# A sparse graph layer on one core: seven units multiply one dense tile of g fewer, and its columns move into their gathered lists

## The chip, the cores and the metric

The kernel runs on one NeuronCore of a Trainium2 chip. The metric is device microseconds of one execution; the kernel before takes 1518.41 us (median of 3 runs, 1517.39 to 1519.67). The engines are TensorE (PE, with its weight loads PEld), VectorE (DVE), ScalarE (ACT), GpSimd (POOL) and SyncE (SP).

## The reference

Eight batches of 4096 nodes with 256 features pass through one graph layer. The adjacency `adj` is sparse: node i is linked to node j with a probability that falls as the square root of both numbers, so the first nodes have by far the most links.

```python
HW     = einsum('bnf,fo->bno', x, W)                # 8 x 4096 x 256
A_norm = relu((adj + adj.T) * 0.5)                  # 4096 x 4096
D      = sum(A_norm, axis=1)
L_norm = eye(4096) - D**-0.5[:, None] * A_norm * D**-0.5[None, :]
out    = relu(einsum('nm,bmo->bno', L_norm, HW))
return layernorm(x + out, axis=-1)
```

The inputs come from a fixed seed, so the pattern of the adjacency is always the same one. Everything is float32.

## The kernel before

It works in two phases. In the **first phase** it reads `adj` in 512x512 tiles, symmetrises them on PE and DVE, writes the result to `a_dram`, and forms g = r * (x W), where r is the inverse root of a node's degree. g has 4096 rows of 2048 values (8 KB: eight batches times 256 features) and is written to `g_dram`. Beside this, PE multiplies row block 0 with all of g (`lead`, L584).

In the **second phase** the other 31 blocks of 128 output rows follow in 16 **units** of two blocks (unit 15 has one), in the order `SEQ` = 1 to 9, 0, 10 to 15. A unit needs only those rows of g whose node is linked to one of its 256 output rows. They are gathered:

- The first `HUBS[u]` tiles of g (a tile is 128 rows; tiles 0 and 1 are almost full) stay in SBUF as `g_hub0` and `g_hub1` and are multiplied densely, with a 128x128 piece of the adjacency that POOL loads for each block (`gh`, L1019, 64 KB).
- All other linked rows go into lists. Each node has a kind: which of the unit's eight groups of 32 output rows it is linked to. `KINDS` names 15 kinds: one group alone (eight kinds), two neighbouring groups, one whole block (15 and 240), or anything (0). `CAPS[u]` gives each kind so many half tiles of 64 places, `FIRST[u]` says where they begin. What does not fit into a kind's places moves on to the kind for pairs, for a block, and last to "anything". A place that stays free is read out of bounds and moves no data. If even that list is too short, a flag makes a complete dense recomputation follow (L1335).
- For each tile of 128 places POOL issues two gathers: the adjacency rows `ga` (L1031) and the g rows `g` (L1039). They go into a ring of 12 buffers; `gather_ahead` issues the next one when the oldest buffer has been used for the last time. Buffers come free in order.

`steps_of` (L877) is the planner for PE. A **step** is what fills the PE array once for all four 512-wide pieces of the output row: a hub tile or a tile of kind 15, 240 or 0 times one block (four full 128x128 matmuls), or a packed **round**, in which up to eight smaller products (64 rows, or 32 or 64 columns) run side by side in the array. `weave` mixes them; the first step of a unit is hub 0 for block 0, the first step of the second block is hub 0 again, and the other hub products are spread between the rounds. A float32 matmul shows as two instructions in the trace.

The queues are ordered by hand (`queue`, `tc.issue_after`). On POOL the gathers and the `gh` loads stand in the order in which the steps release their buffers. ACT evicts the finished blocks (L787) and then issues the loads of the two residual rows `xr` of the next unit (1 MB each); DVE adds, normalises and builds the lists for later units (L238 to L480), PE counts for it (L299, L396, L449), and SP stores each finished block (1 MB).

Lines that matter here: `HUBS`, `CAPS` and `FIRST` (L26 to L64), `steps_of` (L877), `load_hub_rows` (L1012), `gather` and `gather_ahead` (L1024 to L1063), the product (L1254).

Of the kernel before, what the change touches and what calls it, by code (L numbers as in the profile page):

```python
# [22 lines left out]

SEQ = [*range(1, 10), 0, *range(10, 16)]

HUBS = [2] * 16  # L26

CAPS = [
# [16 lines left out]
]  # L45
# [18 lines left out]
]  # L64
# [3 lines left out]
def kernel(  # L68
# [180 lines left out]
    def patterns(u):  # L249

        def t(shape, name, dtype=F32, **kw):
            return ipool.tile(shape, dtype, tag=name, name=f"{name}_{u}", **kw)
# [13 lines left out]
        nc.vector.tensor_tensor(diag, diag, own[:, :, :nb], ALU.max)  # L266
        if HUBS[u]:
            nc.vector.memset(used[:, :, : HUBS[u]], 0.0)
        several = t([P, NB], "several", bufs=1)
# [607 lines left out]
    def steps_of(u):  # L877
# [60 lines left out]
        def full(t, b):  # L938
            return [(t, None, b, 0, QU)]

        def weave(*several):
            several = [list(s) for s in several]
            total = [len(s) for s in several]
            out = []
            while any(several):
                at = max(range(len(several)), key=lambda k: (len(several[k]) / max(total[k], 1), total[k]))
                out.append(several[at].pop(0))
            return out

        held = range(HUBS[u])  # L950
        out = [full(-1, 0)] if HUBS[u] else []
        starts = [full(t, 0) for t in whole[15]]
# [4 lines left out]
        out += weave(rounds[:first_b1], [full(-1 - h, 0) for h in held[1:]], starts)  # L957
        out += [full(-1, 1)] if HUBS[u] else []
        rows = [[full(t, 0), full(t, 1)] for t in whole[0]]
# [13 lines left out]
    with (  # L973
# [5 lines left out]
            gath.enter_context(tc.tile_pool(name=f"hub_{h}", bufs=1)).tile([P, G], F32, name=f"g_hub{h}")  # L979
            for h in range(max(HUBS))  # L980
        ]
# [409 lines left out]
```

## Time and profile before

| | |
|---|---|
| median of 3 runs | 1518.41 us |
| the profiled execution | 1526.28 us, span 1524.6 us, mean granted PE clock 0.976 |
| first phase | up to 584.7 us (first step of unit 1 follows at 588) |
| second phase | 584.7 to 1509.8 us: 925.1 us |
| after it | 14.8 us: the last block is evicted, normalised and stored |
| PE busy | 1430.9 us, 94% of the span |
| DMA queues, share of 16 engines | 48.1% POOL (q0), 23.9% SP (q1), 22.5% ACT (q10) |

The bounds of the units are the evictions of their second blocks: unit 3 begins at 734.3, unit 9 ends at 1150.7, unit 0 lasts to 1248.1, unit 13 ends at 1441.4. In a table of stretches each row gives the length, then busy time and number of instructions of PE, PEld, DVE, ACT and POOL, the granted clock, the share of the 16 DMA engines in use and GB/s. The DMA share adds up the times of single packets and can come out a little over 1.

### The profile page before, as it was taken

Reading aid. Unit: us, or ns where it says so; the run is one execution under the profiler, and the core shown is the slowest. Engines: PE = TensorE matmul, PEld = TensorE weight load, DVE = VectorE, ACT = ScalarE, POOL = GpSimd, SP = SyncE. Lnnn points to the kernel's source line nnn. Section 1 sums busy time; section 2 is a strip of 40 time slices with the busy share of each in tenths; the row PEclk is TensorE's granted clock in tenths of the full one; section 3 lists DMA queues with packets and bytes.
Section 4 is the critical chain, followed back from the end, with each engine's and each line's share of the span. In section 5 each row is a group of like instructions: output and inputs, shape, how many; then the busy total and the mean of one; then the engine's idle time right before and its main releaser. Section 6 shows DMA issues by size and latency. Waiting matters only on the chain.

```text
span 1524.6 us, 20569 instructions
## 1 busy us (share of the span) xinstructions
PE 1430.9 (94%) x6768; PEld 759.5 (50%) x6768; DVE 1028.0 (67%) x3010; ACT 369.3 (24%) x462; POOL 744.7 (49%) x1547
## 2 busy tenths in 40 slices
PE   7999988989999999989999989998999999989996
PEld 6777867777777753333333333332333333333332
DVE  5677569789597726074757676886799149879544
ACT  4555544544455430000000101010100010101102
POOL 3444010012133327556667565576476635756663
PEclk9999999989999999999999989999999999999998
DMA  9999999998999999888989899999899969998996
GB/s 349 364 371 387 405 364 363 386 362 329 393 358 326 371 418 362 337 320 328 358 304 371 288 396 348 356 383 413 294 382 358 412 206 372 364 347 299 405 396 236
DMA packets 215264, 540.52 MB, mean 355 GB/s; under 512 B 17750, under 2 KB 107526, under 8 KB 180838
## 3 DMA queue, kind: packets, MB, share of 16 engines
q0 software_dynamic: 53808, 281.94, 48.1%
q1 hardware_dynamic: 93200, 126.62, 23.9%
q10 hardware_dynamic: 68144, 130.58, 22.5%
q8 instruction: 56, 0.92, 0.2%
q14 instruction: 56, 0.46, 0.1%
HBM read 425.72 MB, written 136.34 MB: 369 GB/s over the span
## 4 chain that ended last, share of the span: by engine, by line
PE 64%; DVE 14%; DMA 14%; issue 3%; ACT 2%; POOL 1%; another core or an unknown queue 1%; ACTq 0%; DVEq 0%; POOLq 0%
PE py L1254 46%; PE pg L626 8%; DMA a_dram<-sym 7%; PE lead L584 5%; DVE sym L519 4%; DMA xin<-in_x_dram 4%; DMA g<-g_dram,gi 2%; PE xtr L615 2%; PE tr L515 2%; ACT sym L523 1%; DVE sums L526 1%; DVE stats L806 1%; DVE xr L797 1%; PE lists L449 1%; DVE xr L830 1%
## 5 line engine op out<-in xcount | busy, mean ns | idle before, releaser
L1254 PE MATMUL py<-g,ga 128*32 128x512 f32 (+4 forms) x2880 | 651.4, 604 | 16.3 <-issue 11.4
L1254 PEld LDWEIGHTS py<-g,ga 128*32 128x32 f32 (+4 forms) x2880 | 230.5, 138 | 408.3 <-issue 389.8
L1039 POOL DMA_INDIRECT g<-g_dram,gi x256 | 288.9, 1128 | 164.3 <-issue 74.3
L1031 POOL DMA_INDIRECT ga<-a_dram,ai x256 | 271.7, 1061 | 159.4 <-issue 59.9
L787 ACT ACTIVATE y<-py,minus_r 128x512 f32<-128x512 f32 x120 | 81.0, 687 | 824.7 <-PE py L1254 598.8
L1254 PE MATMUL py<-g_hub,gh 128*128 128x512 f32 x496 | 234.5, 614 | 13.5 <-DVE low L464 6.6
L626 PE MATMUL pg<-w_sb,xt 128*128 128x256 f32 x1024 | 231.7, 385 | 7.9 <-ACT xt L616 7.7
L626 PEld LDWEIGHTS pg<-w_sb,xt 128*128 128x128 f32 x1024 | 195.8, 194 | 35.5 <-ACT xt L616 8.7
L519 DVE TENSOR_TENSOR sym<-tr,adj 128x512 f32<-128x512 f32 x256 | 162.2, 683 | 60.6 <-PE tr L515 51.1
L526 DVE TENSOR_REDUCE sums<-sym 128x64 f32<-128x2048 f32 x64 | 145.5, 2279 | 64.4 <-ACT sym L523 64.4
L1254 PEld LDWEIGHTS py<-g_hub,gh 128*128 128x128 f32 x496 | 92.3, 194 | 142.3 <-issue 127.2
L527 POOL TENSOR_SCALAR uses<-sums 128x64 uint8<-128x64 f32 x64 | 26.7, 417 | 268.4 <-DVE sums L526 234.9
L515 PE MATMUL tr<-ident,adj 128*128 128x128 f32 x1024 | 137.7, 282 | 19.2 <-DVE sym L519 14.0
L523 ACT ACTIVATE sym<-sym 128x2048 f32<-128x2048 f32 x64 | 122.7, 1918 | 122.4 <-DVE sym L519 118.3
L515 PEld LDWEIGHTS tr<-ident,adj 128*128 128x128 f32 x1024 | 115.6, 143 | 50.4 <-DVE sym L519 31.5
L241 DVE TENSOR_TENSOR_SCAN incl_r<-carry,lists 128x32 f32<-128x32 bf16 x13 | 2.9, 220 | 164.9 <-PE lists L396 164.9
L428 DVE TENSOR_TENSOR hot<-iota_q,at 128x1024 bf16<-128x1024 f32 x64 | 74.6, 1219 | 33.9 <-ACT y L787 32.1
L797 DVE TENSOR_TENSOR xr<-xr,y 128x2048 f32<-128x2048 f32 x31 | 70.8, 2284 | 38.9 <-ACT y L787 34.3
L615 PE MATMUL xtr<-ident,xin 128*128 128x128 f32 x512 | 71.9, 291 | 18.9 <-DVE sym L519 9.8
L830 DVE TENSOR_SCALAR xr<-xr,mv,root 128x256 f32<-128x256 f32 x248 | 84.3, 412 | 1.1
L806 DVE BATCH_NORM_STATS2 stats<-xr 128x6 f32<-128x256 f32 x248 | 84.0, 412 | 1.1
L584 PE MATMUL lead<-gt,strip 128*128 128x512 f32 x176 | 82.4, 593 | 0.0
(164 smaller groups left out, 1038.4 us busy)
## 6 DMA issues: line engine op xcount, KB each, us to landing
adj<-in_adj_dram SPq DMA_DIRECT2D x64, 1024.0 KB
a_dram<-sym ACTq DMA_DIRECT2D x64, 1024.0 KB
out_dram<-xr SPq DMA_DIRECT2D x31, 1024.0 KB
xr<-in_x_dram ACTq DMA_DIRECT2D x28, 1024.0 KB
xin<-in_x_dram SPq DMA_DIRECT2D x44, 512.0 KB
g_dram<-gt ACTq DMA_DIRECT2D x22, 1024.0 KB
xin<-in_x_dram POOLq DMA_DIRECT2D x20, 512.0 KB
g_dram<-held ACTq DMA_DIRECT2D x10, 1024.0 KB
```

What stands on the lines that cost most here:

```text
L515: ins = nc.tensor.transpose(pt[:, c * P : (c + 1) * P], tji[:, c, a * P : (a + 1) * P], ident)
L519: nc.vector.tensor_add(sym[:, a, :], pt, tij[:, a, :])
L523: nc.scalar.activation(sym, sym, AF.Relu, scale=0.5)
L526: nc.vector.tensor_reduce(sums, sym.rearrange("p a (c q) -> p a c q", q=E), AX.X, ALU.add)
L584: nc.tensor.matmul(lead[c], lhsT=strip, rhs=g[:, c * S : (c + 1) * S], start=not done, stop=len(done) == NB - 1, skip_group_check=True,)
L615: nc.tensor.transpose(pt[:, k, c, :], xin[b // H][:, b % H + k, c * P : (c + 1) * P], ident)
L626: ins = nc.tensor.matmul(pg[:, k * FO : (k + 1) * FO], lhsT=xt[:, b + k, c, :], rhs=w_sb[:, c, :], start=(c == 0), stop=(c == FC - 1),)
L806: nc.vector.bn_stats(stats[:, b, :], z[:, b, :])
L830: nc.vector.tensor_scalar(z[:, b, :], z[:, b, :], mv[:, b, 0:1], rstd[:, b : b + 1], ALU.subtract, ALU.mult,)
L1031: nc.gpsimd.indirect_dma_start(out=at if both else at[:, : E if one else P], out_offset=None, in_=a_pairs if both else a_groups if one els ...
L1039: nc.gpsimd.indirect_dma_start(out=gt, out_offset=None, in_=g_dram, in_offset=bass.IndirectOffsetOnAxis(ap=gi[:, t : t + 1], axis=0), boun ...
L1254: return nc.tensor.matmul(py[2 * u + 1 + b][c][cols, :], lhsT=at[ps, off + cols.start : off + cols.stop], rhs=gt[ps, c * S : (c + 1) * S], ...
```

## The change

Only three tables differ. `HUBS` is 1 instead of 2 for units 3, 7, 8, 10, 11, 12 and 13: their two products with `g_hub1` (one for each block) go, and so do the `gh` loads for them. The rows of g in tile 1 that these units need go into the lists, and `CAPS` and `FIRST` of the seven units are laid out anew. Nothing else of the program is edited; the planner draws up the steps, the gathers and the queues from the tables.

```diff
@@ -23,23 +23,23 @@
 
 SEQ = [*range(1, 10), 0, *range(10, 16)]
 
-HUBS = [2] * 16
+HUBS = [2, 2, 2, 1, 2, 2, 2, 1, 1, 2, 1, 1, 1, 1, 2, 2]
 
 CAPS = [
     [5, 4, 4, 4, 4, 2, 2, 2, 2, 3, 2, 2, 2, 2, 12],
     [3, 3, 3, 3, 3, 3, 3, 3, 3, 3, 2, 2, 2, 2, 6],
     [2, 3, 3, 3, 3, 3, 3, 3, 3, 2, 2, 2, 2, 2, 4],
-    [2, 3, 3, 2, 3, 3, 3, 2, 3, 2, 2, 2, 2, 2, 4],
+    [3, 3, 3, 2, 2, 3, 3, 2, 2, 3, 2, 2, 2, 2, 4],
     [2, 3, 3, 2, 3, 3, 3, 3, 2, 2, 2, 2, 2, 2, 2],
     [4, 2, 2, 2, 2, 2, 2, 2, 2, 2, 2, 2, 2, 2, 2],
     [1, 2, 2, 2, 2, 2, 2, 2, 2, 1, 2, 2, 2, 2, 4],
-    [2, 3, 2, 2, 3, 3, 2, 2, 3, 2, 2, 2, 0, 2, 2],
+    [2, 4, 4, 4, 4, 2, 2, 2, 2, 2, 0, 0, 2, 2, 4],
+    [2, 2, 2, 2, 2, 2, 2, 2, 2, 2, 2, 2, 2, 2, 2],
+    [2, 2, 2, 2, 2, 2, 2, 2, 2, 2, 2, 2, 0, 2, 2],
     [0, 2, 2, 2, 2, 2, 2, 2, 2, 2, 2, 2, 2, 0, 4],
+    [0, 2, 2, 2, 2, 2, 2, 2, 2, 2, 2, 2, 2, 2, 2],
     [2, 2, 2, 2, 2, 2, 2, 2, 2, 2, 2, 2, 0, 2, 2],
-    [1, 2, 2, 2, 2, 2, 2, 2, 2, 1, 2, 2, 2, 2, 2],
-    [1, 3, 3, 3, 3, 3, 3, 3, 3, 1, 0, 0, 0, 0, 4],
-    [1, 3, 3, 3, 3, 3, 3, 3, 3, 1, 0, 0, 0, 0, 4],
-    [1, 2, 2, 2, 2, 2, 2, 2, 2, 1, 2, 2, 0, 2, 2],
+    [3, 2, 2, 2, 2, 2, 2, 2, 2, 3, 0, 0, 0, 0, 4],
     [2, 2, 2, 2, 2, 2, 2, 2, 2, 2, 0, 0, 0, 0, 4],
     [6, 2, 2, 2, 2, 0, 0, 0, 0, 0, 0, 0, 0, 0, 0],
 ]
@@ -48,17 +48,17 @@
     [0, 8, 16, 12, 20, 32, 36, 34, 38, 5, 24, 26, 28, 30, 40],
     [24, 0, 12, 6, 18, 3, 15, 9, 21, 27, 30, 32, 34, 36, 38],
     [32, 0, 12, 6, 18, 3, 15, 9, 21, 34, 24, 26, 28, 30, 36],
-    [30, 0, 6, 18, 12, 3, 9, 28, 15, 32, 20, 22, 24, 26, 34],
+    [12, 0, 6, 18, 20, 3, 9, 30, 32, 15, 22, 24, 26, 28, 34],
     [30, 0, 6, 18, 12, 3, 15, 9, 28, 32, 20, 22, 24, 26, 34],
     [24, 0, 4, 2, 6, 16, 20, 18, 22, 28, 8, 10, 12, 14, 30],
     [0, 2, 6, 4, 8, 18, 22, 20, 24, 1, 10, 12, 14, 16, 26],
-    [26, 0, 14, 12, 6, 3, 24, 22, 9, 28, 16, 18, 0, 20, 30],
+    [28, 0, 8, 4, 12, 20, 24, 22, 26, 30, 0, 0, 16, 18, 32],
+    [24, 0, 4, 2, 6, 16, 20, 18, 22, 26, 8, 10, 12, 14, 28],
+    [22, 0, 4, 2, 6, 14, 18, 16, 20, 24, 8, 10, 0, 12, 26],
     [0, 0, 4, 2, 6, 14, 18, 16, 20, 22, 8, 10, 12, 0, 24],
+    [0, 0, 4, 2, 6, 16, 20, 18, 22, 24, 8, 10, 12, 14, 26],
     [22, 0, 4, 2, 6, 14, 18, 16, 20, 24, 8, 10, 0, 12, 26],
-    [0, 2, 6, 4, 8, 18, 22, 20, 24, 1, 10, 12, 14, 16, 26],
-    [24, 0, 12, 6, 18, 3, 15, 9, 21, 25, 0, 0, 0, 0, 26],
-    [24, 0, 12, 6, 18, 3, 15, 9, 21, 25, 0, 0, 0, 0, 26],
-    [0, 2, 6, 4, 8, 16, 20, 18, 22, 1, 10, 12, 0, 14, 24],
+    [0, 6, 10, 8, 12, 14, 18, 16, 20, 3, 0, 0, 0, 0, 22],
     [16, 0, 4, 2, 6, 8, 12, 10, 14, 18, 0, 0, 0, 0, 20],
     [8, 0, 4, 2, 6, 0, 0, 0, 0, 0, 0, 0, 0, 0, 0],
 ]
```

What the tables make of it, by running the planner on both and by counting the links of the reference's adjacency (rows: linked rows of g that are gathered, out of the places of the unit's tiles):

| unit | steps before, now | of them hub | tiles | rows gathered |
|---|---|---|---|---|
| 3 | 17, 16 | 4, 2 | 19, 19 | 2128, 2248 |
| 7 | 14, 13 | 4, 2 | 16, 18 | 1874, 1976 |
| 8 | 14, 12 | 4, 2 | 14, 15 | 1778, 1880 |
| 10 | 13, 12 | 4, 2 | 14, 14 | 1680, 1775 |
| 11 | 12, 11 | 4, 2 | 15, 14 | 1594, 1688 |
| 12 | 12, 11 | 4, 2 | 15, 14 | 1569, 1664 |
| 13 | 12, 11 | 4, 2 | 13, 13 | 1537, 1632 |
| all 16 | 234, 226 | 62, 48 | 256, 257 | 29952, 30655 |

No list of either kernel is too long for its places (the tightest, "anything" of unit 11, holds 127 of 128), so the dense recomputation runs in neither.

On PE, unit 13 shows it. Before, after the first round on gathered tiles, the step with hub tile 1 stands ahead of the first step of the second block (`py_0` is the unit's first block, `py_1` its second; the index behind it is one of the four 512-wide pieces):

```order
L1254 MATMUL py_0_3_11760<-g_5771,ga_5783 32x512
L1254 MATMUL py_0_0_11757<-g_hub_5723,gh_0_5786 128x512
L1254 MATMUL py_0_1_11758<-g_hub_5723,gh_0_5786 128x512
L1254 MATMUL py_0_2_11759<-g_hub_5723,gh_0_5786 128x512
L1254 MATMUL py_0_3_11760<-g_hub_5723,gh_0_5786 128x512
L1254 MATMUL py_1_0_11850<-g_hub_5719,gh_1_5785 128x512
L1254 MATMUL py_1_1_11851<-g_hub_5719,gh_1_5785 128x512
L1254 MATMUL py_1_2_11852<-g_hub_5719,gh_1_5785 128x512
L1254 MATMUL py_1_3_11853<-g_hub_5719,gh_1_5785 128x512
```

Now a step with a gathered tile of a whole block stands there:

```order
L1254 MATMUL py_0_3_11672<-g_5713,ga_5758 32x512
L1254 MATMUL py_0_0_11669<-g_5717,ga_5759 128x512
L1254 MATMUL py_0_1_11670<-g_5717,ga_5759 128x512
L1254 MATMUL py_0_2_11671<-g_5717,ga_5759 128x512
L1254 MATMUL py_0_3_11672<-g_5717,ga_5759 128x512
L1254 MATMUL py_1_0_11765<-g_hub_5705,gh_1_5771 128x512
L1254 MATMUL py_1_1_11766<-g_hub_5705,gh_1_5771 128x512
L1254 MATMUL py_1_2_11767<-g_hub_5705,gh_1_5771 128x512
L1254 MATMUL py_1_3_11768<-g_hub_5705,gh_1_5771 128x512
```

The step that needed no gather is gone; the one in its place needs the fifth gather of the unit.

On POOL, at the first gathers of unit 13 (the rows of `g` and `ga` with `gi` 11309 before, 11224 now, behind the last of unit 12), stands before:

```order
L1031 DMA ga_5779<-a_dram,ai_10872 128x32
L1039 DMA g_5755<-g_dram,gi_10870 128x2048
L1031 DMA ga_5780<-a_dram,ai_11311 128x32
L1039 DMA g_5759<-g_dram,gi_11309 128x2048
L1019 DMA gh_0_5786<-a_dram 128x128
L1019 DMA gh_1_5785<-a_dram 128x128
L1031 DMA ga_5781<-a_dram,ai_11311 128x32
L1039 DMA g_5763<-g_dram,gi_11309 128x2048
```

and now:

```order
L1031 DMA ga_5766<-a_dram,ai_10836 128x32
L1039 DMA g_5745<-g_dram,gi_10834 128x2048
L1031 DMA ga_5767<-a_dram,ai_11226 128x32
L1039 DMA g_5749<-g_dram,gi_11224 128x2048
L1031 DMA ga_5768<-a_dram,ai_11226 128x32
L1039 DMA g_5753<-g_dram,gi_11224 128x2048
L1031 DMA ga_5769<-a_dram,ai_11226 128x32
L1039 DMA g_5757<-g_dram,gi_11224 128x2048
```

Before, two loads of hub pieces stand between the first and the second tile of the unit; now the first three tiles follow each other without one. Over the whole program POOL issues 14 such loads fewer and two gathers (one tile) more.

## The prediction

> **What bounds the kernel now.** I read the page first, then the second phase in stretches, then single instructions and the waits. The page, with the engines, the queues and the chain that ended last:
>
> ```profile
> PE 1430.9 (94%) x6768; PEld 759.5 (50%) x6768; DVE 1028.0 (67%) x3010; ACT 369.3 (24%) x462; POOL 744.7 (49%) x1547
> q0 software_dynamic: 53808, 281.94, 48.1%
> q1 hardware_dynamic: 93200, 126.62, 23.9%
> q10 hardware_dynamic: 68144, 130.58, 22.5%
> PE 64%; DVE 14%; DMA 14%; issue 3%; ACT 2%; POOL 1%; another core or an unknown queue 1%; ACTq 0%; DVEq 0%; POOLq 0%
> ```
>
> PE is busy for 94% of the span, but the three queues together fill 48.1 + 23.9 + 22.5 = 94.5% of the DMA engines. Two resources stand close together, and the change takes work from the one and gives it to the other. So the stretches decide. These are units 1 and 2; 3 to 9; 0; 10 to 13; 14 and 15:
>
> ```profile
> core 0: us, PE busy (x) PEld busy (x) DVE busy (x) ACT busy (x) POOL busy (x), PEclk, DMA share, GB/s
> 584.70:734.30 149.60, 143.13 (x643) 53.77 (x643) 76.99 (x268) 8.54 (x13) 96.31 (x92) 0.97 0.86 329
> 734.30:1150.70 416.40, 397.67 (x1710) 147.97 (x1712) 311.20 (x1119) 37.85 (x56) 267.59 (x256) 0.97 0.95 357
> 1150.70:1248.10 97.40, 97.03 (x368) 37.91 (x364) 43.90 (x160) 5.50 (x8) 56.17 (x56) 1.00 0.87 330
> 1248.10:1441.40 193.30, 186.88 (x926) 74.35 (x922) 156.16 (x558) 21.57 (x32) 126.93 (x121) 1.00 0.95 350
> 1441.40:1509.80 68.40, 65.12 (x220) 25.66 (x216) 31.27 (x114) 8.29 (x13) 37.65 (x35) 1.00 0.97 376
> ```
>
> In the two stretches that hold the changed units (second and fourth row) PE is idle for 18.7 and 6.4 us, and the DMA engines have only 5% to spare: 21 and 10 us. What PE itself waited for, in the second stretch and then in the last one:
>
> ```profile
> PE py L1254 <- issue: 8.1, 13, 1.2
> PE py L1254 <- DVE low L464: 6.6, 1, 6.6
> PE py L1254 <- DMA g<-g_dram,gi: 1.1, 1, 1.1
> ...
> PE py L1254 <- DMA g<-g_dram,gi: 2.7, 1, 2.7
> PE py L1254 <- DMA gh<-a_dram: 0.6, 1, 0.6
> ```
>
> Up to unit 13 the gathers come in time: 1.1 us of waiting in 416. Only from unit 14 on is PE held by them; there the chain of waits leaves PE and runs through the gathers until the last unit:
>
> ```profile
> 1446.63 1.94 POOL ga L1031
> ...
> 1454.36 12.19 DMA g<-g_dram,gi
> ...
> 1468.55 12.02 DMA g<-g_dram,gi
> ...
> 1484.26 10.32 DMA gh<-a_dram
> ```
>
> So **PE bounds units 1 to 13, with the transfers just behind it, and the transfers bound the end**.
>
> **What the change removes on PE.** The plan has 234 steps before and 226 now: one fewer in units 3, 7, 10, 11, 12 and 13, two in unit 8. What a step costs does not depend on its kind:
>
> ```profile
> 1254.12 3.64 PE L1254 MATMUL py<-g,ga 128*32 128x512 f32 x32
> 1257.69 7.13 PE L1254 MATMUL py<-g_hub,gh 128*128 128x512 f32 x16
> 1264.76 21.42 PE L1254 MATMUL py<-g,ga 64*128 64x512 f32 x80
> ```
>
> The first row is one round of four 32-column products, the second two hub steps, the third the next six steps of unit 10, packed and full ones: 21.42 / 6 = 3.57 us a step. The 14 hub steps removed are thus worth 14 x 3.57 = 50.0 us, the six other steps that the new lists need in their place cost 21.4, and 8 x 3.57 = **28.6 us** of PE time are left: 14.3 in units 3, 7 and 8, 14.3 in units 10 to 13.
>
> **What it adds on the DMA engines.** The seven units gather 120 + 102 + 102 + 95 + 94 + 95 + 95 = 703 rows more, of 8 KB each: 5.76 MB. The price is that of queue q0: 48.1% of 1524.6 us for 281.94 MB, 2.60 us a MB, so 15.0 us. By the plan the adjacency rows beside them grow from 14.5 to 15.0 MB (more places are shared by both blocks), 1.2 us. Fourteen hub pieces of 64 KB are not loaded, 0.92 MB, 2.4 us less. Net **+13.8 us of all 16 engines**: 324 of the rows and 6 pieces in the second stretch, 6.9 - 1.0 + 0.5 = +6.4; 379 rows and 8 pieces in the fourth, 8.1 - 1.4 + 0.7 = +7.4.
>
> **What is free.** POOL issues 14 loads fewer and one pair of gathers more, and it is busy for 64 to 66% of these stretches. DVE builds lists of other lengths (three instructions more) and sets some constants in the first phase; there it is 0 to a microsecond. DVE's cover is PE: were PE to run 3.5 us shorter in each unit, DVE, 311 of 416 us busy, would still not be the bound. ACT and SP do what they did. The first phase does not change.
>
> **The sum.** In the second stretch PE alone would need 416.4 - 14.3 = 402.1 us, and the transfers need 0.95 x 416.4 + 6.4 = 402.0 us at a share of 1: a dead heat. In the fourth PE would need 193.3 - 14.3 = 179.0 and the transfers 0.95 x 193.3 + 7.4 = 191.0. Both ends of the price therefore hang on one number, the share that the engines reach when PE no longer holds them back. The lowest that I take is the present 0.95: 423.2 and 201.1 us, together 14.6 us slower than now. The highest is what the trace shows over 60 us of unit 0, the queues' shares there:
>
> ```profile
> DMA packets 6763, 24.69 MB, mean 412 GB/s; under 512 B 842, under 2 KB 3920, under 8 KB 4352
> q0 software_dynamic: 3724, 21.59, 87.3%
> q1 hardware_dynamic: 1926, 1.94, 9.2%
> q10 hardware_dynamic: 1109, 1.11, 5.4%
> ```
>
> That is 102%: the second stretch is then PE's 402.1, the fourth 187.3, together 20.3 us faster. Full use over hundreds of microseconds is not to be had, since the ring of 12 buffers fills and empties; but the present 5% are mostly places where a full ring waits for PE, and these go first. I take **0.985**, nearer to the upper end: 408.1 (-8.3) and 193.9 (+0.6). The other stretches keep their plan, and the last one its bound. Sum: **-8 us**, nearly all of it from units 3, 7 and 8; units 10 to 13 give back as transfers what PE saves. The profiled execution took 1526.28 us, 0.5% over the median; I take the 8 us off the median: 1518.4 - 8 = **1510 us**.
>
> A page that speaks against the change: the Trainium skill, "DMA: Bandwidth & Descriptors", section "Where 436 GB/s comes from", says that for transfers to or from HBM the HBM side, about 358 GB/s for one core, is the limit. By that rule the second stretch, at 357, would be full today and every added byte would cost its time, an estimate of 6.4 us there; the 412 GB/s above over 60 us say that here it is not so.
>
> **What a new wait costs beyond itself.** The rows below are unit 8's first step, at 2 us, 9 us and 5 us, and for comparison 25 us of unit 6:
>
> ```profile
> 1042.00:1044.00 2.00, 1.92 (x5) 0.57 (x3) 2.00 (x7) 0.00 (x0) 1.66 (x2) 1.00 1.02 425
> 1044.00:1053.00 9.00, 2.21 (x4) 0.59 (x4) 0.62 (x4) 0.19 (x1) 5.78 (x7) 0.90 1.02 411
> 1053.00:1058.00 5.00, 4.71 (x18) 1.27 (x22) 4.34 (x34) 2.23 (x4) 2.56 (x3) 0.50 1.02 417
> 940.00:965.00 25.00, 25.00 (x98) 9.52 (x91) 20.80 (x65) 0.00 (x0) 17.96 (x17) 1.00 1.03 396
> ```
>
> With the transfers at 1.02, PE, DVE and ACT nearly stand still for 9 us, and then the granted clock is 0.50 for 5 us: 6.8 + 2.5 = 9.3 us lost. What stopped them I cannot tell; unit 6 works on undisturbed at 1.03, so a full share is a condition for it at most, not the cause. The Trainium skill, "TensorE: Matmul & The Clock Gate", section "HAM oscillation — how this bites in real kernels", states that a wait for transfers of more than about 3.4 us throttles PE to half its clock; the third row agrees (0.50 behind the wait).
>
> **The rivals.**
> *PE's saving comes through in the second stretch, and the fourth gains too* (share 1.0 to 1.02): -17 to -20 us, about 1499. For it: the gathers' slack up to unit 13, and unit 0 without a changed plan, where the share falls to 0.87 and the ring fills again. Against it: the fourth stretch, whose gathers have no slack left at its end.
> *Slower: the transfers become the bound, in units 3 to 13.* One mechanism: the share does not rise above about 0.96, because POOL issues a gather only when the oldest buffer is free, and the lists now lie denser, so a late tile holds all that stand behind it. Then the stretches last 418.8 and 199.0, +8 us: 1526. It decides from a share below 0.973, where the sum, 413.2 + 196.3 = 609.5, meets today's 609.7. One more event like that of unit 8 moves the border by 9 us and does the same.
> *Nothing to be measured*: a share of about 0.975, or the forecast and one such event.
> *The change doesn't do what it says* by a list that overflows, which would start the dense recomputation. By the count of links it can't; I give it nothing.
>
> **How the numbers follow.** The forecast has a chance of 0.42, PE's full saving 0.20, no change (within 0.2%, 3 us, about what a measurement of this kernel can tell) 0.18, slower 0.20. Faster by more than 0.2% is the first two: 0.62. The range reaches from 1497, just under the rival of 1499 (0.08 lies below), to 1523, four fifths of the way from the forecast to the slower case (0.12 above). The forecast's own range is 1504 to 1514.
>
> **What would show it.** Right: the steps still take 3.5 to 3.6 us; the second stretch is some 8 us shorter with a DMA share of 0.98 or more; the stretch of units 10 to 13 is as long as before within 4 us and now has PE waiting for g, which it doesn't before; q0 moves 5.3 MB more. Wrong: a share that stays at 0.95 with PE waits on g in units 4, 8 and 9 (the units behind those that grew denser), more events of 9 us with a clock of 0.50, or a fourth stretch that shrinks by more than 6 us.

## The result and the profile after

The changed kernel takes **1504.9 us** (median of 4 runs, 1499.9 to 1506.6), the kernel before beside it 1518.7 (1517.4 to 1519.7): ratio 0.990, 95% interval 0.988 to 0.993, or 10.8 to 18.4 us faster. The forecast was 8 us. The time lies in the stated range, but the gain is larger than forecast: 8 lies below the interval. Where the gain came from was forecast wrongly.

The page of the changed kernel: engines, the three queues, the chain that ended last.

```profile
PE 1406.1 (93%) x6584; PEld 746.6 (50%) x6584; DVE 1028.0 (68%) x3020; ACT 369.3 (25%) x462; POOL 741.5 (49%) x1521
...
q0 software_dynamic: 53552, 287.25, 49.1%
q1 hardware_dynamic: 93200, 126.62, 24.3%
q10 hardware_dynamic: 68144, 130.58, 22.7%
...
PE 60%; DVE 19%; DMA 12%; issue 5%; ACT 3%; POOL 1%; another core or an unknown queue 0%; ACTq 0%; DVEq 0%; POOLq 0%
```

PE is busy for 25 us less and q0 moves 5.31 MB more, both as forecast. But q0's share, 49.1% of 1504.0 us, is 738 us of the engines against 733 before: 5 us more where 15 were expected. The stretches, from here on from the first product of a unit to that of the next (units 1 and 2; 3 to 9; 0; 10 to 13; 14 and 15):

```profile
core 0: us, PE busy (x) PEld busy (x) DVE busy (x) ACT busy (x) POOL busy (x), PEclk, DMA share, GB/s
582.70:734.60 151.90, 145.25 (x649) 54.68 (x648) 79.58 (x279) 9.44 (x16) 97.43 (x94) 0.97 0.87 331
734.60:1139.80 405.20, 384.27 (x1685) 141.73 (x1683) 310.39 (x1120) 38.28 (x57) 268.58 (x251) 0.97 0.96 366
1139.80:1240.30 100.50, 99.28 (x368) 39.04 (x364) 43.56 (x159) 5.53 (x10) 62.41 (x62) 1.00 0.91 344
1240.30:1420.10 179.80, 170.52 (x782) 64.06 (x778) 155.44 (x557) 21.48 (x34) 121.39 (x111) 0.98 1.02 393
1420.10:1491.60 71.50, 67.83 (x218) 26.20 (x216) 32.33 (x115) 8.49 (x13) 34.44 (x34) 0.95 0.91 348
```

The second and the fourth row answer to 416.40 (0.95, 357) and 193.30 (0.95, 350) in the prediction. Units 3 to 9 are 11 us shorter at hardly more DMA share. Units 10 to 13, to which the forecast gave nothing, are **13.5 us shorter**, at 1.02. Units 0, 14 and 15 give back 6 us. These rows add up to 19 us, since the profiled execution of before was itself 8 us above its median. Single executions scatter (33 of the kernel before in one group of runs below: 1511 to 1527 us), so the total is read from the ratios and the traces are read for what repeats in all of them.

What PE waited for in units 10 to 13:

```profile
PE lists L449 <- DVE pos_r L246: 6.5, 2, 4.3
PE py L1254 <- DMA g<-g_dram,gi: 1.5, 1, 1.5
```

The waits for g that were to swallow PE's saving there are 1.5 us. PE's longest waits in these units are now for DVE, which builds the lists.

### The profile page after: what moved, and what is told of

It reads as the page before. It is cut to its first block, busy times and chain, and to the rows that moved or that the text cites. A ratio compares the mean times of both kernels' runs of the same rounds, so it can differ in the third digit from the quotient of the medians.

```text
span 1504.0 us, 20175 instructions
## 1 busy us (share of the span) xinstructions
PE 1406.1 (93%) x6584; PEld 746.6 (50%) x6584; DVE 1028.0 (68%) x3020; ACT 369.3 (25%) x462; POOL 741.5 (49%) x1521
## 3 DMA queue, kind: packets, MB, share of 16 engines
q0 software_dynamic: 53552, 287.25, 49.1%
## 4 chain that ended last, share of the span: by engine, by line
PE 60%; DVE 19%; DMA 12%; issue 5%; ACT 3%; POOL 1%; another core or an unknown queue 0%; ACTq 0%; DVEq 0%; POOLq 0%
PE py L1254 40%; PE pg L626 9%; DMA a_dram<-sym 7%; PE lead L584 5%; DVE sym L519 4%; DMA g<-g_dram,gi 3%; PE xtr L615 3%; PE tr L515 3%; ACT sym L523 2%; DVE stats L806 1%; DVE sums L526 1%; DVE hot L428 1%; DVE xr L830 1%; DVE xr L797 1%; DMA xin<-in_x_dram 1%
## 5 line engine op out<-in xcount | busy, mean ns | idle before, releaser
L1254 PE MATMUL py<-g,ga 128*128 128x512 f32 (+4 forms) x2808 | 678.4, 605 | 23.0 <-issue 16.1
L1254 PEld LDWEIGHTS py<-g,ga 128*128 128x128 f32 (+4 forms) x2808 | 236.6, 140 | 427.5 <-issue 401.1
L1039 POOL DMA_INDIRECT g<-g_dram,gi x257 | 297.4, 1157 | 149.4 <-issue 77.3
L1254 PE MATMUL py<-g_hub,gh 128*128 128x512 f32 x384 | 182.5, 616 | 5.5 <-issue 3.4
L1254 PEld LDWEIGHTS py<-g_hub,gh 128*128 128x128 f32 x384 | 71.6, 194 | 111.7 <-issue 104.4
```

The source lines that it names most:

```text
L1039: nc.gpsimd.indirect_dma_start(out=gt, out_offset=None, in_=g_dram, in_offset=bass.IndirectOffsetOnAxis(ap=gi[:, t : t + 1], axis=0), boun ...
L1254: return nc.tensor.matmul(py[2 * u + 1 + b][c][cols, :], lhsT=at[ps, off + cols.start : off + cols.stop], rhs=gt[ps, c * S : (c + 1) * S], ...
```

## The experiments

The kernel before took 1468 us in the first group of runs, 1518 in the second and third and 1506 in the fourth; why it moves by 3% between groups is not known (the record gives the chip of the first and of the fourth group the same number, so the chip's number doesn't tell), and each kernel is compared with the kernel before of its own group only. The **lists** of a unit are here its rows of the three tables, with the tiles and the order of the steps that the planner makes of them. All are built from the two kernels by exchanging rows of the tables or by the edits shown.

### First group (the kernel before: 1468.06 us, 1464.95 to 1473.22): halves and parts

Units 3, 7 and 8 alone, and units 10 to 13 alone: the kernel before with the other one's rows of the three tables.

```diff
 HUBS, CAPS, FIRST:
+rows 3, 7, 8 of the changed kernel           (early)
+rows 10, 11, 12, 13 of the changed kernel    (late)
```

> The change in units 3, 7 and 8 alone: 4 steps fewer (14.3 us of PE), 324 rows more. As the prediction had it, nearly the whole gain lies here: -8 us. If every removed step is worth its 3.57 us wherever it lies, less a few us of waits, and rows cost little, half of the measured gain lies here: -6 to -10 us. If the gain came from the new layout of the late lists, 0.

Measured: 1478.78 us, ratio **1.0073** (1.0054 to 1.0092). Slower by 10.7 us; none of the three expectations holds.

> The change in units 10 to 13 alone: 4 steps fewer (14.3 us of PE), 379 rows more. As the prediction had it, the transfers give back here what PE saves: 0, at most -3 us. If a removed step is worth its time wherever it lies: -6 to -12 us, and with the run on units 3, 7 and 8 it adds up to the whole change, -13.8.

Measured: 1467.34 us, ratio 0.9988 (0.9978 to 0.9999), up to 3 us faster, as the prediction had it for these units.

The steps without the rows: tables as before, eight hub products of tile 1 and their `gh` loads left out (so part of the output is missing).

```diff
+    DROP = {(3, -2, 1), (7, -2, 1), (8, -2, 0), (8, -2, 1), (10, -2, 1), (11, -2, 1), (12, -2, 1), (13, -2, 1)}
     def steps_of(u):
+        return [step for step in planned(u) if not any((u, op[0], op[2]) in DROP for op in step)]
...
-            u = next((v for v in units if HUBS[v] > h and blocks(v) > b), None)
+            u = next((v for v in units if HUBS[v] > h and blocks(v) > b and (v, -1 - h, b) not in DROP), None)
```

> The kernel before, with eight products with hub tile 1 left out (the second block's in the seven units, and also the first block's in unit 8), and their loads of hub pieces: 8 steps fewer at the places of the change, no row more; the output lacks these eight products. If PE bounds all the way to unit 13: -28.6 us less the waits that come forward, -20 to -28. If the transfers are the bound of units 10 to 13, as predicted: -14 to -17.

Measured: 1470.78 us, ratio 1.0013 (0.9995 to 1.0030). Eight steps of 3.57 us gone from PE, and not a microsecond gained. Both expectations fall: the smaller one was 14 us.

The rows without the steps: in units 3, 7, 10 and 13 the free places of the lists load a row too, instead of being skipped.

```diff
+        if u in (3, 7, 10, 13):
...
+            nc.vector.tensor_scalar(flag[:, :t], low[:, :t], float(N), None, ALU.is_ge)
+            nc.vector.scalar_tensor_tensor(free[:, :t], flag[:, :t], iota_p, low[:, :t], ALU.mult, ALU.add)
+            nc.vector.scalar_tensor_tensor(free[:, :t], flag[:, :t], float(3 * P - N), free[:, :t], ALU.mult, ALU.add)
+            nc.vector.tensor_copy(gi[:, :t], free[:, :t])
+        else:
...
```

> The kernel before, whose 717 free places in the lists of units 3, 7, 10 and 13 are read from real rows of g instead of being skipped (their adjacency rows are zero, so the result is the same): the transfers of the change without its PE saving, 717 rows against 703. At the full price of queue q0 it is 15 us of the engines, of which the 5% to spare hide most: 0 to +4 us. If rows are dear beyond their share (a late tile holds all behind it): +8 to +15. DVE does three instructions of 0.2 us more in each of four units.

Measured: 1471.94 us, ratio 1.0023 (1.0010 to 1.0035). 5.87 MB more than the 281.94 of before cost the kernel 3.4 us (1.5 to 5.1), **0.6 us a MB** (0.25 to 0.9). That is the expectation of 0 to +4, in which most of the engines' added time is hidden; it doesn't speak against the 2.6 us a MB of the prediction, which is time of the engines. Queue q0 on the page of this kernel, and on that of the steps-only kernel beside it:

```profile
q0 software_dynamic: 53808, 287.81, 49.9%
```

```profile
q0 software_dynamic: 53552, 281.42, 48.7%
```

Of spans of 1470.2 and 1470.1 us these are 734 and 716 us of the engines: 18 us for 6.39 MB, 2.8 us a MB.

### Second group (the kernel before: 1518.31 us, 1505.22 to 1525.51): the whole again, and a second trace of before

> The kernel before, unchanged, for a trace of it on the chip that the experiments have. The four experiments so far ran on a chip (or in a place of one) where the kernel before takes 1468 us, 50 us less than where the change was measured. If the two places differ in what bounds units 1 to 13, the trace shows it: in the slower one the rows of g landed about 20 us before their first use in units 3 to 9 (median by unit 15.9 to 28.5 us), and steps of 9 to 12 us stood at the starts of units 2, 3, 4, 5 and 8 where nothing was late. Theory P (PE bounds both places): slack again 15 us or more in units 2 to 9. Theory D (in the faster place the stalls of units 2 to 5 are gone and PE has caught up with the gathers): slack 4 to 10 us in units 2 to 9, and no step above 8 us in units 3 to 5.

Measured: theory P's slack. The median by unit, from the landing of a tile's last packet to its first product, was 16.0 to 28.5 us in units 3 to 9, and the long steps at the starts of units 2 to 5 were there again (10.2, 9.6, 8.4 and 9.8 us). In the first group's traces of the two halves and of the steps the slack of these units was 6.5 to 17.3 us, and steps over 8 us in units 3 to 5 were absent.

> The whole change beside the kernel before on the same chip. If it lands in the faster place (before about 1468 us): theory P, that each of the eight steps left out is worth 3.5 us minus some of the rows, as it was in the slower place, expects -14 us. Theory D, that there the gathers bound units 1 to 13, expects what its two halves gave there alone: +10.7 us of units 3, 7 and 8 and -0.7 us of units 10 to 13, together about +10 us (1.007), with the loss in units 3 to 9 and with the slack of the gathers near zero there. If it lands in the slower place (before about 1518 us), both expect -14 us again.

Measured: 1500.98 us, ratio **0.9895** (0.9860 to 0.9929). It repeats. The whole change was not measured where the kernel before takes 1468 us: that stays open.

### Third group (the kernel before: 1517.49 us, 1510.97 to 1526.94): the parts where the whole gains

> Units 3, 7 and 8 changed alone, as in e1_early, which came out 0.7% slower where the kernel before takes 1468 us. The whole change was measured twice where the kernel before takes 1518 us, at 0.990 and 0.990. Theory P (where the kernel before takes 1518 us the gathers of units 2 to 9 land 15 to 28 us before their use, so a step left out is time gained; where it takes 1468 us they land 4 to 10 us before it and a gain of PE is waited away): about -8 us at 1518, about +10 us at 1468. Theory L (these three units' new lists, three tiles more, lose by themselves wherever they run): slower than before in both places, and the whole change's gain comes from units 10 to 13 alone.

Measured: 1517.29 us, ratio **0.9986** (0.9964 to 1.0007). No gain to be told apart from none. Theory P expected -8; theory L, in the form that these lists lose by themselves, expected a slower kernel, which is not seen here either.

> Units 10 to 13 changed alone, as in e2_late, which came out at 0.999 where the kernel before takes 1468 us. Theory P: -6 to -9 us where the kernel before takes 1518 us, about -1 us at 1468. Theory L: the whole change's -14 to -17 us and some more at 1518. The recorded prediction gave these units nothing (+0.6 us).

Measured: 1506.76 us, ratio **0.9918** (0.9890 to 0.9946): -8 to -17 us. The expectation of theory L, the whole -14 to -17 us and more, is met at the upper end of the interval only. The two halves give -0.14% and -0.82%, the whole -1.05%: within their intervals the gain is that of units 10 to 13.

> The eight steps left out and nothing put into the lists, as in e3_steps_only (this kernel leaves out the products of eight hub blocks), which gained nothing where the kernel before takes 1468 us. Theory P: -20 to -28 us where the kernel before takes 1518 us, so that what lies between this and the whole change (-14 to -17 us) is the price of the rows there; about +2 us again at 1468. Theory L: no difference to the whole change at 1518.

Measured: 1514.95 us, ratio **0.9978** (0.9950 to 1.0006): -8 to +1 us. Theory P, that PE's time counts wherever the gathers are early, falls: it expected -20 to -28. What is recorded for theory L here, the time of the whole change, falls as well. So, of the change's two sides, what gains is not what it takes from PE.

The last kernel of this group tries the long steps at the unit starts, told in the last section:

```diff
-                    with queue("act"):
-                        xr[i] = residual(i, nc.scalar)
+                    with queue("sp"):
+                        xr[i] = residual(i, nc.sync)
```

> The whole change with the loads of xr issued on SP's queue behind the stores, instead of on ACT's queue beside them. In the traces the long steps at the starts of units 2 to 5 (7 to 12 us, nothing late, all engines slow) stand where a load of xr and a store of xr run at the same time as the gathers, each with a sixth of the DMA time, at a share of 1.01 to 1.05. If three queues at once are the cause, these steps shrink below 6 us and the kernel gains 10 to 30 us on the whole change where the kernel before takes 1518 us; where it takes 1468 us, without such steps, it changes nothing. If the full share alone is the cause, or something outside these queues, the steps stay and the time is the whole change's within 5 us; if the loads come too late behind the stores, PE or DVE waits for xr and it is slower.

Measured: 1521.95 us, ratio 1.0020 (0.9986 to 1.0054), 18 to 20 us above the whole change, were that at 0.990 in this group too (it was not run there). The long steps stayed (9.9, 9.1, 11.0 and 9.0 us in units 2 to 5), and DVE now waited for the loads, 39 us in three places. Three queues at once are not the cause of these steps; the other side of the expectation, loads that come too late, is what happened.

### Fourth group (the kernel before: 1505.88 us, 1497.99 to 1520.45): the steps put back

The whole change with the eight products of tile 1 run as well (their columns then count twice in the output).

```diff
+    PUT = [(3, -2, 1), (7, -2, 1), (8, -2, 0), (8, -2, 1), (10, -2, 1), (11, -2, 1), (12, -2, 1), (13, -2, 1)]
+    def held_of(u, b):
+        return range(HUBS[u] + ((u, -2, b) in PUT))
...
-            [full(-1 - h, 1) for h in held[1:]],
+            [full(-1 - h, 1) for h in held_of(u, 1)[1:]],
...
```

> The new lists of all seven units with the eight steps put back: their eight products of the second hub block (of b=1, in unit 8 of both) run as well, so the kept columns of the second tile count twice in the output. 234 steps, as before, and the rows and tiles of the whole change. With the kernel before (old lists, 234 steps), the steps-only kernel (old lists, 226 steps: -2.5 us where the kernel before takes 1518 us) and the whole change (new lists, 226 steps: -14 to -17 us) this fills the square. Theory G (with the old lists the gathers of units 11 to 13 set the pace, so a step left out is waited away; the new lists, two tiles fewer there, supply PE in time, and only then a step left out is time gained): putting the steps back costs most of 8 x 3.5 us on the whole change, +8 to +14 us on the kernel before. Theory L (the lists gain by themselves, through fewer tiles to gather; the steps are worth as little here as with the old lists): +2 to +4 us on the whole change, so -10 to -14 us on the kernel before.

Measured: 1495.74 us, ratio **0.9932** (0.9899 to 0.9964).

> The whole change again, beside the kernel with the steps put back. Where the kernel before takes 1518 us: 0.990 for a third time. Where it takes 1468 us: the sum of its two halves there, +10.7 and -0.7 us, gives 1.007; if the halves do not add up (units 10 to 13 profit from what units 3, 7 and 8 leave out) it lies between 0.99 and 1.00.

Measured: 1497.51 us, ratio **0.9931** (0.9904 to 0.9959). With 234 steps or with 226, the new lists gain the same: 28.6 us of steps put back cost no more than the intervals leave, some 6 us. Theory G, 8 to 14 us slower than before, falls; theory L holds: **the gain is the lists'**. It is a little smaller in this group (10 us) than in the second (16), within the intervals.

## What the lists do: the traces

Units 10 to 13 in six kernels, one row each. Old lists: the kernel before, early alone, the steps-only kernel.

```profile
core 0: us, PE busy (x) PEld busy (x) DVE busy (x) ACT busy (x) POOL busy (x), PEclk, DMA share, GB/s
1241.60:1436.50 194.90, 188.46 (x926) 72.97 (x922) 154.78 (x549) 21.45 (x33) 127.65 (x121) 0.98 0.96 350
```

```profile
1236.70:1430.70 194.00, 189.57 (x923) 75.17 (x923) 154.63 (x550) 21.48 (x33) 128.01 (x122) 0.98 0.96 353
```

```profile
1237.00:1435.20 198.20, 181.53 (x894) 66.90 (x891) 154.21 (x549) 19.71 (x30) 131.16 (x123) 0.96 0.94 354
```

New lists: late alone, the whole again, the whole with the steps put back.

```profile
1242.70:1423.10 180.40, 171.35 (x783) 65.87 (x779) 154.42 (x556) 21.21 (x33) 121.73 (x111) 0.98 1.02 392
```

```profile
1239.80:1419.70 179.90, 170.37 (x781) 63.76 (x779) 155.02 (x557) 21.03 (x33) 123.21 (x113) 0.98 1.02 396
```

```profile
1229.40:1411.30 181.90, 179.28 (x814) 68.38 (x810) 155.49 (x556) 21.11 (x33) 128.90 (x118) 1.00 1.02 401
```

194 to 198 us with the old lists, 180 to 182 with the new ones, whatever PE has to do; the third row has four steps fewer and is the longest, the last row has four more than the two above it and costs 2 us. Share times length, the time that the transfers need, is 183 to 187 us in all six, although the new lists bring 379 rows, 3.1 MB, more. What differs is the time in which the 16 engines stand partly idle. Adding it up from the packets, in bins of 4 us, gives for these units 11 to 12 us in the two traces of before and in early alone, 15 for the steps alone; up to 2 us for late alone, the whole change and the steps put back. The first group's traces say the same: 7 (early), 8 (steps only), 1 (late). By unit, it is unit 12 that shrinks most: from 53.4 and 55.2 us in the two traces of before to 41.4, 45.1 and 46.5 in the three of the whole change. Unit 11 goes from 47.8 and 48.0 to between 44.5 and 47.4, and units 10 and 13 change by less than 4 us.

The holes stand in the same places in all four traces of these groups with old lists: at the ends of units 10, 11 and 12, and at unit 12's step of eight packed products. In the second trace of before:

```profile
1281.60:1289.60 8.00, 8.00 (x65) 3.04 (x61) 7.49 (x33) 0.00 (x0) 5.59 (x6) 1.00 0.87 317
1329.60:1337.60 8.00, 8.00 (x45) 3.65 (x38) 7.49 (x33) 1.77 (x3) 2.47 (x3) 1.00 0.56 199
1361.60:1377.60 16.00, 15.81 (x91) 5.78 (x88) 15.38 (x44) 2.64 (x4) 12.74 (x10) 0.98 0.79 277
1385.60:1393.60 8.00, 8.00 (x39) 3.84 (x38) 7.12 (x42) 2.41 (x4) 3.03 (x3) 1.00 0.85 295
```

PE is busy throughout in all four: while the engines run dry, PE waits for nothing. POOL's own rows there show two different reasons. First the first, the second and the fourth hole:

```profile
1282.48 1.06 POOL L1031 DMA_INDIRECT ga<-a_dram,ai  x1 [3.80 <-PE py L1254]
...
1334.52 1.00 POOL L1039 DMA_INDIRECT g<-g_dram,gi  x1 [6.60 <-PE lists L449]
...
1389.71 1.08 POOL L1039 DMA_INDIRECT g<-g_dram,gi  x1 [5.33 <-PE lists L449]
```

POOL stands for 3.8, 6.6 and 5.3 us, each time until PE releases it: the ring is full. A gather takes the buffer of the tile twelve places back, and only in order. How many buffers each step of unit 12 sets free follows from the plan (first h for a hub step, otherwise the number of products in the step; then the buffers that it frees):

```
old:  h 0 | 4 4 | h 0 | h 0 | 2 1 | 1 0 | 1 0 | 8 0 | 1 1 | 4 0 | 1 9 | h 0
new:  h 0 | 4 4 | 1 1 | 2 0 | h 0 | 1 0 | 2 0 | 2 2 | 1 2 | 1 1 | 4 4
```

Unit 11's old row is the same. Five steps free one buffer, then one frees nine at once: the engines first run dry and then have nine tiles to fetch. The third hole has another reason. POOL is busy there for 12.74 of 16 us and waits for no buffer; the transfers are held to its pace. That pace, 20 us earlier:

```profile
1343.52 0.94 POOL L1031 DMA_INDIRECT ga<-a_dram,ai  x1 [0.30 <-issue]
1344.77 1.01 POOL L1039 DMA_INDIRECT g<-g_dram,gi  x1 [0.30 <-issue]
1346.08 0.95 POOL L1031 DMA_INDIRECT ga<-a_dram,ai  x1 [0.30 <-issue]
```

A tile costs POOL 2.56 us here, whether it has 128 rows (issued at 1339.64) or 71 (at 1342.20). The four tiles of unit 12 that it issues from 1342 to 1350 hold 71, 104, 84 and 93 rows: 88 x 8 KB in 2.56 us is 280 GB/s, as long as no other queue fills the engines. In the hole itself POOL is slower still:

```profile
1362.39 2.08 POOL L1039 DMA_INDIRECT g<-g_dram,gi  x1 [1.15 <-DMA g<-g_dram,gi]
1364.78 1.87 POOL L1031 DMA_INDIRECT ga<-a_dram,ai  x1 [0.30 <-issue]
1366.96 1.35 POOL L1039 DMA_INDIRECT g<-g_dram,gi  x1 [0.30 <-issue]
1368.95 2.43 POOL L1031 DMA_INDIRECT ga<-a_dram,ai  x1 [0.64 <-issue]
```

Why these instructions take up to 2.43 us instead of 0.94 to 1.01 is not known; they hold 84 and 96 rows a tile and come 4.6 us apart. The old lists of units 10 to 13 put 6380 rows into 57 tiles, 112 a tile; the new ones 6759 into 55, **123 a tile**. In units 3, 7 and 8 it is 5780 in 49 and 6104 in 52, 118 and 117: nothing improves there, three tiles are added, and near its end unit 3's new plan has steps that free 0, 3, 0 and then 8 buffers. The idle time of the engines goes from 7 us to none in unit 8, but from 6 to 7 up to 9 to 10 in unit 3 and from none to 3 in unit 7 (two traces each). That fits a half that gains nothing.

That the lists make the gain is shown by the kernels. That they make it through these two things, evenly freed buffers and fuller tiles, is argued from traces: neither was changed alone. And a step of the argument is missing, for in the kernel before PE does not wait for g in units 10 to 13 at all. Its waits there, in the first trace:

```profile
PE py L1254 <- issue: 4.1, 6, 0.8
PE lists L449 <- DVE pos_r L246: 1.7, 3, 0.8
```

What it loses in these units against 3.53 us a step, 20 and 22 us in the two traces, sits in long steps. The largest are the fourth and the fifth step of unit 12, a hub step and the round behind it (6 and 8 us together), and the rounds of eight products in units 11 and 12 (5 us together); none of them had a tile that landed less than 6 us before. With the new lists and the steps put back these long steps are absent and the loss is 9 us. So a rival stands: the new lists may gain because their steps don't run into such stalls, whose cause is open (last section). Waiting for gathers shows in the steps-only kernel, where PE is ahead: 5.4 us for a tile of g at the start of unit 13, right behind the lump at the end of unit 12, and its loss there is 39 us. In the whole change it is 21 to 22 us over four steps fewer, 7 of them waits for DVE in the first trace. These rows alone would also fit a gain of four steps of PE; it is the two kernels with the other number of steps that rule that out.

The whole second phase, from unit 1's first product to the last, by the same traces. Counted at 3.53 us a step, the commonest length of a step with nothing in its way (the median of all is 3.58), what the phase has beyond that is PE's loss.

| kernel | lists | steps | second phase, us | PE's loss | time of the transfers |
|---|---|---|---|---|---|
| before, two traces | old | 234 | 927.7, 928.0 | 101.5, 101.9 | 859, 863 |
| steps only | old | 226 | 916.4 | 118.5 | 854 |
| whole, three traces | new | 226 | 908.9, 907.9, 904.4 | 111.0, 110.0, 106.5 | 862, 858, 858 |
| whole, steps put back | new | 234 | 897.5 | 71.3 | 858 |

The transfers take 854 to 863 us in each. With either lists PE loses more when it has less to do. These are single executions of three groups: the last row's was 6 us under its median, the third of the whole change 6 us over, so of the 35 us between them some 12 are scatter.

## Why the prediction was right in its range and wrong in its reasons

That the time came near is luck: the -8 us were put on units 3, 7 and 8, which alone gave nothing that could be told from zero, and units 10 to 13, which were to give nothing, gave 8 to 17 us.

**"PE bounds units 1 to 13, with the transfers just behind it", so that a step removed is time gained: wrong, and the step that failed.** I read it from the absence of waits: 1.1 us on g in 416. The absence is real, but it doesn't show a bound. With the old lists eight steps could go (-0.2%, -0.5 to +0.1) and with the new ones they could come back (0.993 against 0.993) without a change that the measurement sees. With four steps fewer, units 10 to 13 of the old lists took 198 us instead of 193 to 195: PE lost in late gathers and long steps what it had been spared. And its losses sat in long steps that I had listed as events without a cause.

**"8 x 3.57 = 28.6 us of PE time": right as work** (PE is busy for 25 us less, the median step is 3.57 to 3.58 us in every trace), **worth nothing as time that the measurement sees** (at most 8 us of it, by the interval of the third group). In units 3 to 9 the traces scatter too much to exclude a few us: 404 us with four steps fewer and old lists, 407 to 416 with all.

**"2.60 us a MB, 15.0 us of rows": not what the rows cost here.** By q0's shares its packets took 733 and 734 us in the two traces of before and 738, 732 and 732 in the three of the whole change: 2 us less to 5 us more, where 15 were added in the sum. In the first group the price did come out as engine time (2.8 us a MB), and the kernel paid 0.6. Why the two places differ is open. The transfers of units 10 to 13, which were to need 7.4 us more, need 183 to 184 us instead of 186 to 187.

**"Both ends hang on one number, the share": two numbers, both missed.** 0.985 was taken for both stretches, measured were 0.96 in units 3 to 9 and 1.02 in units 10 to 13, for 180 us, though I had written that full use over hundreds of microseconds is not to be had. I wrote that the missing 5% "are mostly places where a full ring waits for PE, and these go first". They are: at three of the four holes POOL waits for PE. But a faster PE does not remove them, since the steps of a unit free the buffers in lumps at any speed. In the steps-only kernel, where PE is four steps faster, the share fell to 0.94.

**"Nearly all of it from units 3, 7 and 8; units 10 to 13 give back": the wrong way round.** Alone they gave -0.1% (0.9964 to 1.0007) and -0.8% (0.9890 to 0.9946).

**"POOL ... is busy for 64 to 66% of these stretches": an average over stretches.** In the middle of unit 12 the transfers go at its pace.

**The rivals.** PE's full saving (-17 to -20) came near in time and is wrong as a mechanism. The slower one, a ring in which late tiles hold the rest, named the right object with the wrong sign: the old lists were the lumpy ones in units 11 and 12. It fits what units 3, 7 and 8 do, and where the kernel before takes 1468 us the early half alone is slower by 10.7 us. In that trace PE waits for g in units 3 to 9 and 0:

```profile
PE py L1254 <- DMA g<-g_dram,gi: 10.9, 7, 2.7
```

There the late half gains next to nothing (0 to 3 us), though its units 10 to 13 show the same 1.02:

```profile
1202.60:1382.10 179.50, 170.23 (x782) 64.08 (x778) 154.90 (x556) 21.98 (x32) 125.70 (x111) 0.98 1.02 395
1382.10:1451.90 69.80, 66.64 (x220) 26.10 (x216) 32.77 (x115) 8.28 (x13) 36.26 (x34) 0.98 0.92 353
```

In the steps-only kernel of the same group units 10 to 13 take 191.6 us, 12 more. But its units 14 and 15 take 62.9 us, 7 less than in the second row, and its unit 0 takes 97.4 instead of 102.2: the gain is given back before and behind these units, half of it in a step of 10.4 us at unit 14's start, whose fourth tile lands 1.5 us late.

**What was to show it.** Steps of 3.5 to 3.6 us and 5.3 MB: right. Units 3 to 9 at 0.98 or more: wrong, 0.96. Units 10 to 13 as long as before with PE waiting for g: wrong, and it is the sign that I had named for being wrong, "a fourth stretch that shrinks by more than 6 us".

**The limit of 358 GB/s.** Units 10 to 13 moved 392 to 401 GB/s for 180 us. The Trainium skill, "DMA: Bandwidth & Descriptors", section "Where 436 GB/s comes from", has about 358 as the binding side for transfers with HBM; the measurement decides, and it is 10 to 12% above. The same page, section "Measured (HBM→SBUF, 128 partitions, SWDGE, issued from GpSimd)", says that such figures hold with the pair's other core idle and that each gets about 358 when both stream. Whether a neighbour was what moved the kernel before between 1468 and 1518 us, no run here can show.

## What to carry to other kernels

A busy engine that waits for nothing is not yet the bound: leave some of its work out, and put it back beside the other half of the change; if the time stays both times, the gain is elsewhere. For gathers through a ring of buffers, count from the plan how many buffers each step frees and how full each tile is: here a tile took the issuing engine 2.56 us with 128 rows and with 71, and behind a step that freed nine buffers at once the transfers had run dry. Added time of the DMA engines is not yet added time of the kernel: add the bytes alone and measure both.

## What was not expected of the hardware

In units 2 to 5 single steps take 7 to 12 us, in all traces where the kernel before takes 1506 to 1518 us and hardly in those where it takes 1468. One of them in the changed kernel, unit 5's second step, and below it the weight loads on PE, with the idle time before each:

```profile
870.40:882.40 12.00, 7.87 (x34) 1.86 (x34) 2.44 (x17) 0.00 (x0) 8.11 (x10) 0.86 1.02 392
```

```profile
874.55 0.11 PEld L1254 LDWEIGHTS py<-g,ga 128*32 128x32 f32 x1 [1.31 <-issue]
875.97 0.11 PEld L1254 LDWEIGHTS py<-g,ga 128*32 128x32 f32 x1 [1.31 <-issue]
876.68 0.11 PEld L1254 LDWEIGHTS py<-g,ga 128*32 128x32 f32 x1 [0.61 <-issue]
878.11 0.11 PEld L1254 LDWEIGHTS py<-g,ga 128*32 128x32 f32 x1 [1.33 <-issue]
```

The tiles of this step had landed 4 us and more before, and yet PE gets a weight load only every 0.7 to 1.4 us; DVE's instructions beside it, most of 0.16 to 0.18 us, stand up to 1.9 us apart, while POOL keeps its pace until 880. The same place in the late half, in the group where the kernel before takes 1468 us, has a share no lower and no loss (that step takes 3.6 us; the row begins in its middle):

```profile
841.60:848.60 7.00, 7.00 (x32) 2.71 (x25) 6.56 (x27) 0.00 (x0) 5.50 (x5) 1.00 1.04 415
```

So a full share alone isn't the cause, nor are three queues at once (the serial kernel). No transfer that the profile calls instruction lies in these 12 us (the nearest begin at 859.9 and 899.7). What it is stays open. The two long steps of unit 12 with the old lists look alike: the first multiplies a hub tile that lies in SBUF, and in the second trace of before it takes 8.4 us at a share of 1.04. It isn't a constant loss either: with the steps put back, units 7 to 14 had no step above 5.6 us, and PE's loss over the phase was 71 us against 107 in the whole change of the same group, where the work that was added is 28 and the scatter of the two executions 12.
